# A graph kernel whose first attention block is gathered during the list stage

## The chip, the cores and the metric

The kernel runs on one core of one Trainium2 chip, in one launch. The metric is device time in microseconds (us). A core has TensorE (PE, matmuls), VectorE (DVE), ScalarE (ACT), GpSimd (POOL) and SyncE (SP); each works through its own instructions in order, and semaphores tie them together. Sixteen DMA engines move data between the chip's memory (HBM) and the core's on-chip memory (SBUF); PSUM is the memory that PE writes to. SP and ACT issue plain DMAs. POOL issues indirect ones, called gathers here: a gather fetches, for each of 128 partitions, one row of a table in HBM whose number stands in an index tile.

## The reference

Two graph layers over 4096 nodes with 512 features and an adjacency matrix `adj` of 4096 x 4096 whole numbers, in which about one entry in a thousand is 1, so that a node has some four neighbours.

```python
# layer 0: attention with 8 heads of 64
Wh = jnp.einsum('nf,hfo->hno', x, W)
f1 = jnp.einsum('hno,ho->hn', Wh, a[:, :64]);  f2 = jnp.einsum('hno,ho->hn', Wh, a[:, 64:])
e = jax.nn.leaky_relu(f1[:, :, None] + f2[:, None, :], 0.2)
e = jnp.where(adj[None] > 0, e, -9e15)
out = jnp.einsum('hnm,hmo->hno', softmax(e), Wh)        # heads side by side: 4096 x 512
x = layernorm(x + out)
# layer 1: mean over neighbours
agg = (adj > 0) @ x / max(deg, 1)
out = relu(concat([x @ W_self + b_self, agg @ W_nb + b_nb]) @ W_comb + b_comb)
x = layernorm(x + out)
```

## The kernel before

It never multiplies by the adjacency matrix. It turns each row of the matrix into a short list of neighbours and then gathers only the rows that are listed. (A second function, `dense_layers`, runs only if a list overflows; it does not run on these inputs.) Work is cut into 32 blocks of 128 nodes (`NB`, `P`).

**The list stage** (loop at the end of `listed_layers`, `for b in range(LB)`, 27 steps). A step does three things. It takes a block of x, transposes it on PE (`transposed`, L353, copied out by ACT, L355), multiplies by W (`node_half`, L361), and writes a row of 528 numbers for each node into the HBM table `t0`: 8 numbers f2, 512 of Wh, 8 of f1 (`store`, L970, on POOL's queue; the last block's on SP's). It masks a block of `adj` on ACT (`mask_adj`, L425) from two loads of 1 MB (`load_adj`, L419, on SP), and PE and DVE fold it into keys (`fold_adj`, L444; `max_keys`, L459). And every fourth step, `decode` unpacks four blocks of keys on DVE into lists. In five steps (`AHEAD`) two node blocks are done, so that t0 is written in 27 steps while five adjacency blocks are left; one of them, block 27, is folded just after. The x blocks stay in `xs`, one slot for each, for both layers' residuals; `load_x` (L347) runs eight blocks ahead. POOL copies small parts of each row (`node_rest`, L388 to L390), stores the row, and adds it to a running sum (`add_row`, L398), from which the mean row is made (L408) and stored as the last row of t0; nodes without neighbours point to it.

**Slots.** Block b has `KS` = 5 index columns `idx[:, b, k]`: slot 0 is each node's first neighbour, and slots 1 to 4 are shared: each serves 32 of the block's 128 nodes, and holds their further neighbours packed one after another. Which node owns an entry of a shared slot is a 0/1 matrix (`own`), and a matmul with it adds the entry to its owner.

**Early and late lists.** `late_lists` (L563, on steps 12 to 16) makes second lists for blocks 0 to 5 (`NE`), for layer 1: `idxe` is `idx` with every entry from a limit on replaced by a row of padding, so that layer 1 can gather its first blocks before the last rows are written, and `idxl` is one more slot per block with the neighbours left out, whose owners stand in `esl`. For block 0 the limit is row block 25 (`LE`). In layer 0 these lists are not used.

**Layer 0** (`for i in range(-3, NB + 2)`) is a pipeline written out by hand. Step i gathers block i+6 (L626, five gathers, one for each slot), computes the attention weights of block i+3 (`a_weights`, L658; `a_exp`, L666), multiplies the gathered rows of block i+2 by them (`a_weigh`, L676; `a_first`, L684), adds the shared slots' rows of block i+1 to their owners on PE (`a_shared`, L701, 16 small matmuls) and finishes them with residual and moments (`a_recip`, `a_scale`, `a_moments`, L709 to L723), normalizes block i on ACT (L731 to L740), and multiplies block i-1 by the folded weights of layer 1 (`a_z`, L745), whose result goes to the HBM table `t1` (L750); the transposed block is stored too (L753). There are five gather buffers (`GA`), so the gathers of a block wait until `a_shared` of the block five before is done. Blocks 0, 1 and 2 are gathered before the loop. The four adjacency blocks that are left, 28 to 31, are loaded in quarters of 512 KB into two weight tiles that are still free (`load_late`, L945) and masked (`mask_late`, L961) at the end of the steps that `MASKS` names; after a block's fourth quarter, the next step folds it. After the last of them, `TURN` starts their `decode` and loads the self weights.

**Layer 1** gathers five slots of t1 for each block, with seven buffers (L626 again), blocks 0 to 5 early and with one late slot, and multiplies each block's transposed rows by the folded self weights (L771, into the PSUM tiles `nm` and `pw` in turn) and adds the shared slots to their owners (L778).

The order on each engine is that of the program text (`manual_schedule`); the framework adds the waits. For DMAs of SP and ACT together it has eight semaphores, which are used in turn, so a DMA waits for the one eight before it; POOL's DMAs have eight of their own.

The start sets the first loads. These lines come before the list stage:

```python
    for h in range(H):
        nc.sync.dma_start(
            w_sb[:, :, H + h * D : H + (h + 1) * D], w0[h].rearrange("(c p) o -> p c o", p=P)
        )
    load_x(0, nc.scalar)
    brw = load_bias()
    load_x(1)
    load_adj(0, ap)
```

Of the kernel before, what the change touches and what calls it, by code (L numbers as in the profile page):

```python
# [31 lines left out]
F32 = mybir.dt.float32  # L32
# [81 lines left out]
def listed_layers(  # L114
# [35 lines left out]
    FIRST = (0, 1, 3, *range(LB + 1, NB))  # L150

# [114 lines left out]
    esl = const.tile([P, NE, 2], F32, name="esl")  # L266
    endl = const.tile([P, NE + 8], F32, name="endl")[:, 0:NE]
# [77 lines left out]
    def load_x(b, eng=nc.sync):  # L345
        if b < NB:
            eng.dma_start(xs[:, b, :], x[ts(b, P), :])  # L347
# [215 lines left out]
    def late_lists(dp, place):  # L563

        L = lst[:, 0:NE, 0:KL]
        far = lim.unsqueeze(2)
        lv = dp.tile([P, NE, KL], F32, name="lv", bufs=1)
        nc.vector.tensor_tensor(lv, L, far.to_broadcast([P, NE, KL]), OP.is_ge)
        nl = dp.tile([P, 16], F32, name="nl", bufs=1)[:, 0:NE]
# [8 lines left out]
        tl = dp.tile([P, NE, KL + 3], F32, name="tl", bufs=1)  # L578
        nc.vector.tensor_copy(tl, lst[:, 0:NE, 0 : KL + 3])
# [15 lines left out]
        pe = ps.tile([P, NE, KL + 3], F32, name="sm", bufs=2)  # L595
        for b in range(NE):
            nc.tensor.matmul(pe[:, b, :], lhsT=place[:, b, :], rhs=tl[:, b, :], start=True, stop=True)
        el = dp.tile([P, NE, KL + 3], F32, name="el", bufs=1)
        nc.vector.tensor_copy(el, pe)
        nc.vector.tensor_copy(esl, el[:, :, KL + 1 : KL + 3])  # L600
        kx = dp.tile([P, NE], F32, name="kxl", bufs=1)
# [10 lines left out]
        nc.vector.tensor_scalar(idxl, jx, float(N + 1), None, OP.min)  # L612
# [29 lines left out]

    def gather_early(b, pool):
        return gather(t1[0 : 2 + min(LE + b, LX) * P, :], b, pool, idxe)
# [5 lines left out]
    G0, OWN, E, EX0, RD, Y, NM, MV, RS = ({} for _ in range(9))  # L650
# [4 lines left out]

    def a_weights(b, wp):
        e = E[b] = wp.tile([P, KS + 1, H], F32, name="e", bufs=3)[:, 0:KS]
        nc.vector.tensor_add(e, G0[b][:, :, 0:H], f1s[:, b])  # L658
        nc.vector.scalar_tensor_tensor(e, e, SLOPE, e, OP.mult, OP.max)

    def a_exp(b):

        e = E[b]
        EX0[b] = e[:, 0, :]
        w = E[b] = ps.tile([P, KS, H], F32, name="ew")
        nc.scalar.activation(w, e, AF.Exp)  # L666
        nc.scalar.activation(G0[b][:, K0:KS, 0:H], e[:, K0:KS, :], AF.Exp)
# [28 lines left out]
    def a_shared(b):  # L696

        for a in range(2):
            r = slice(a * (H + HH), H + HH + a * HH)
            for k in range(KH):  # L700
                nc.tensor.matmul(  # L701
                    NM[b][ts(k, HP), a * HD : a * HD + r.stop - r.start],
                    lhsT=OWN[b][:, k, :], rhs=G0[b][:, K0 + k, r],
                    start=False, stop=True, tile_position=(0, k * HP), skip_group_check=True,
                )
# [145 lines left out]
    for h in range(H):  # L851
        nc.sync.dma_start(
            w_sb[:, :, H + h * D : H + (h + 1) * D], w0[h].rearrange("(c p) o -> p c o", p=P)
        )
# [16 lines left out]
    xT = transposed(0, wp)  # L871
# [100 lines left out]
    w, lists = 0, []  # L972
    for b in range(LB):
        for k in range(1 + (b in AHEAD)):
            load_x(w + k + XL)
        if b + 2 <= LB:
            load_adj(b + 2, ap)
        if b == 4:
            pads(wp)
        for k in range(2):  # L980
            some(lists)
        ahead = [transposed(w + 1, wp) if w + 1 < NB else None]
        key_bank(b + 1)
        mask_adj(b + 1, 0)

        def then():
            ahead.append(transposed(w + 2, wp))
            mask_adj(b + 1, 1)

        if b not in AHEAD:  # L990
            mask_adj(b + 1, 1)
        row = node_block(
            w, xT, None if ahead[0] is None else b, keep=ahead[0] is None,
            **(dict(then=then) if b in AHEAD else {}),
        )
        w, xT = w + 1, ahead[0]
        if b in AHEAD:
            node_block(w, xT)
            w, xT = w + 1, ahead[1]
        for k in range(2):  # L1000
            some(lists)
        if b % G == G - 1:
            lists = [decode(b + 1 - G, dp, on_own)]
        if b == 12:
            late_nb = late_lists(dp, last)
        if 12 <= b < 17:
            next(late_nb, None)
# [17 lines left out]

    gps = [gather_buffer(0)]
    G0[0] = gather(t0, 0, gps[0])
# [10 lines left out]
    G0[1] = gather(t0, 1, gps[1])  # L1038
# [14 lines left out]
    G0[2] = gather(t0, 2, gps[2])  # L1053
    MASKS = {-1: 2, 0: 2, 1: 1, 2: 1, 3: 2, 4: 1, 5: 1, 6: 2, 7: 1, 8: 1, 9: 2}
# [8 lines left out]
    biased = fold_bias(loaded, bcol[:, FB:])  # L1063
    for i in range(-3, NB + 2):
        if on(i + 1):
            a_shared(i + 1)
        if on(i + 1 + GA):
            G0[i + 1 + GA] = gather(t0, i + 1 + GA, gps[(i + 1 + GA) % GA])
        elif on(i + GA - NB - 1) and i + GA - NB - 1 < GA:
            b = i + GA - NB - 1  # L1070
            G1[b] = gather_early(b, gps[(NB + b) % GA])
        if on(i + 3):
            a_weights(i + 3, wq)
        if on(i + 2):
            a_weigh(i + 2, slice(K0, KS))
# [36 lines left out]
        for k in range(2 if i == 1 else 0):  # L1112
            load_late()
        for k in range(MASKS.get(i, 0)):
# [21 lines left out]
    gps = [gps[(NB + b) % GA] for b in range(GA)]  # L1136
# [480 lines left out]
```

## Time and profile before

| | us |
|---|---|
| median of the runs (3 runs, 632.29 to 635.61) | 632.58 |
| the profiled execution, its own time | 634.25 |
| its span, first to last instruction | 632.5 |
| list stage, to POOL's first gather | 206.9 |
| POOL's last gather starts | 618.6 |
| busy: PE, DVE, ACT, POOL | 555.4, 427.6, 395.7, 395.5 |

Times in the profile count from the span's start. A row of the timeline gives start, duration, engine, line, operation and tiles, and in brackets the idle time of the engine before it with what ended that time ("issue": nothing that the profile shows). A row of the page's groups gives line, engine, operation, count, then busy time in us and the mean of one in ns, and the idle time before. A row of the rates by stage gives for each engine its busy us and number of instructions, then TensorE's granted clock as a share of full speed, the share of time the DMA engines were busy (a little over 1 where packets overlap), and GB/s. DMA-issuing instructions of SP do not count as busy; a gather's time on POOL does, and is the time to issue it, not to land it.

### The profile page before, as it was taken

To read this page: it belongs to the slowest core of one execution; us is meant where nothing else is said; L and a number is where in the kernel's file an instruction comes from. 1 tells how busy PE (TensorE), PEld (TensorE's weight loads), DVE (VectorE), ACT (ScalarE), POOL (GpSimd) and SP (SyncE) were. 2 spreads that over 40 slices of the span, in tenths; PEclk is the share of its full clock that TensorE was granted. 3 is DMA by queue.
4 is the path that set the end of the run, shared out by engine and by line. 5 is a ranking of instruction groups with operands and counts; after the bars stand their busy time and mean duration, and the time that the engine had idled before them with its cause. 6 is when DMAs were issued, how large, how long until landed. Compare 5 with 4: busy or idle time off the path is not lost.

```text
span 632.5 us, 9237 instructions
## 1 busy us (share of the span) xinstructions
PE 555.4 (88%) x2562; PEld 281.8 (45%) x2562; DVE 427.6 (68%) x1176; ACT 395.7 (63%) x891; POOL 395.5 (63%) x503
## 2 busy tenths in 40 slices
PE   7889799888898397989998989988889999999993
PEld 4666576665665233434443434443433333333321
DVE  7237879899799878768999997794024545455422
ACT  2577777668587036878885757775235666766541
POOL 5235344334444777767777777777777777777771
PEclk9889999999999788989999989999999999999997
DMA  8999999999898978999999999999879999999983
GB/s 230 406 408 377 410 407 408 409 408 409 314 374 314 356 218 276 372 405 404 363 368 391 307 293 312 308 290 307 293 226 308 308 330 317 328 325 322 311 272 124
DMA packets 92107, 210.45 MB, mean 333 GB/s; under 512 B 13761, under 2 KB 13769, under 8 KB 92048
## 3 DMA queue, kind: packets, MB, share of 16 engines
q1 hardware_dynamic: 63296, 114.32, 48.6%
q0 software_dynamic: 28560, 95.17, 44.7%
q8 instruction: 23, 0.38, 0.2%
q10 hardware_dynamic: 192, 0.28, 0.2%
q14 instruction: 36, 0.29, 0.1%
HBM read 175.91 MB, written 33.83 MB: 332 GB/s over the span
## 4 chain that ended last, share of the span: by engine, by line
PE 39%; DMA 26%; DVE 23%; ACT 6%; issue 4%; POOL 1%; SPq 1%; DVEq 0%; ACTq 0%; POOLq 0%
DMA at<-in_adj_dram 12%; DMA g<-t,idx 9%; PE pw L771 8%; PE nm L771 8%; PE pw L745 5%; PE pw L361 4%; DVE g L676 3%; PE nm L778 3%; PE pw L778 2%; PE tp L314 2%; PE pw L314 2%; DMA wc<-in_adj_dram 2%; ACT ab L425 2%; DVE lt L528 2%; DVE kk L459 1%
## 5 line engine op out<-in xcount | busy, mean ns | idle before, releaser
L626 POOL DMA_INDIRECT g<-t,idx x290 | 276.3, 953 | 93.5 <-issue 49.4
L361 PE MATMUL pw<-w_sb,xT 128*128 128x264 f32 x496 | 125.7, 400 | 9.6 <-DVE row L365 9.4
L425 ACT ACTIVATE ab<-at 128x2048 bf16<-128x2048 int32 x56 | 106.8, 1908 | 37.8 <-DMA at<-in_adj_dram 32.5
L745 PE MATMUL pw<-wr,xT 128*128 128x512 f32 x256 | 120.4, 614 | 3.3 <-ACT xT L355 3.2
L361 PEld LDWEIGHTS pw<-w_sb,xT 128*128 128x128 f32 x496 | 91.8, 194 | 35.2 <-DVE row L365 12.8
L676 DVE TENSOR_TENSOR g<-g,ew 128x2048 f32<-128x2048 f32 x32 | 73.0, 2283 | 8.2 <-ACT ew L666 8.2
L388 POOL COPY lst<-row 128x8 f32<-128x8 f32 x32 | 6.9, 215 | 114.1 <-DVE row L365 93.2
L745 PEld LDWEIGHTS pw<-wr,xT 128*128 128x128 f32 x256 | 46.9, 193 | 63.9 <-issue 49.8
L771 PE MATMUL pw<-m,xT 128*128 128x512 f32 x128 | 58.9, 603 | 0.0
L771 PE MATMUL nm<-m,xT 128*128 128x512 f32 x128 | 58.8, 602 | 0.0
L355 ACT COPY xT<-tp 128x512 f32<-128x512 f32 x64 | 37.2, 582 | 19.4 <-PE tp L353 19.3
L353 PE MATMUL tp<-ident,xs 128*128 128x128 f32 x256 | 40.7, 284 | 4.9 <-DVE jk L548 2.3
L365 DVE COPY row<-pw 128x264 f32<-128x264 f32 x62 | 26.3, 425 | 27.7 <-PE pw L361 23.2
L353 PEld LDWEIGHTS tp<-ident,xs 128*128 128x128 f32 x256 | 31.6, 146 | 29.0 <-issue 17.7
L398 POOL TENSOR_TENSOR acc<-acc,row 128x528 f32<-128x528 f32 x30 | 39.6, 1319 | 0.6
L794 DVE SCALAR_TENSOR_TENSOR sm<-g,lst,nm 128x512 f32<-128x512 f32 x15 | 11.3, 755 | 41.1 <-PE nm L778 34.3
L771 PEld LDWEIGHTS pw<-m,xT 128*128 128x128 f32 x128 | 23.2, 189 | 35.3 <-issue 26.9
L771 PEld LDWEIGHTS nm<-m,xT 128*128 128x128 f32 x128 | 23.3, 190 | 34.9 <-issue 25.7
L701 PE MATMUL num<-g,own 128*32 128x256 f32 (+1 forms) x512 | 35.6, 396 | 2.9 <-ACT num L694 2.9
L794 DVE SCALAR_TENSOR_TENSOR sm<-g,lst,pw 128x512 f32<-128x512 f32 x15 | 11.3, 755 | 37.2 <-PE pw L778 33.0
L626 POOL DMA_INDIRECT g<-t,idxe x30 | 28.8, 959 | 9.1 <-issue 5.8
L731 ACT ACTIVATE row<-y,ln_sum 128x512 f32<-128x512 f32 x31 | 22.4, 722 | 15.6 <-DVE y L799 15.6
(233 smaller groups left out, 881.2 us busy)
## 6 DMA issues: line engine op xcount, KB each, us to landing
at<-in_adj_dram SPq DMA_DIRECT2D x56, 1024.0 KB
xt<-xT SPq DMA_DIRECT2D x32, 256.0 KB
t<-row SPq DMA_DIRECT2D x32, 256.0 KB
xT<-xt SPq DMA_DIRECT2D x32, 256.0 KB
out_dram<-row SPq DMA_DIRECT2D x32, 256.0 KB
t<-row POOLq DMA_DIRECT2D x31, 264.0 KB
xs<-in_x_dram SPq DMA_DIRECT2D x31, 256.0 KB
m<-in_adj_dram SPq DMA_DIRECT2D x10, 512.0 KB
```

Of the source, the lines that this page charges most:

```text
L353: nc.tensor.transpose(tp[:, c, :], xs[:, b, ts(c, P)], ident)
L355: nc.scalar.copy(t, tp)
L361: nc.tensor.matmul(pw, lhsT=xT[:, c, :], rhs=w_sb[:, c, k * HW : (k + 1) * HW], start=(c == 0), stop=(c == FB - 1),)
L365: nc.vector.tensor_copy(row[:, k * HW : (k + 1) * HW], pw)
L398: nc.gpsimd.tensor_tensor(acc, acc, row, OP.add)
L425: nc.scalar.activation(ab, loads.pop((b, h)), AF.Relu, accum_out=asum[:, b, h : h + 1])
L626: nc.gpsimd.indirect_dma_start(out=out, out_offset=None, in_=table, in_offset=bass.IndirectOffsetOnAxis(ap=at, axis=0),)
L676: nc.vector.tensor_tensor(gv, gv, E[b][:, sl].unsqueeze(3).to_broadcast([P, sl.stop - sl.start, H, D]), OP.mult,)
L701: nc.tensor.matmul(NM[b][ts(k, HP), a * HD : a * HD + r.stop - r.start], lhsT=OWN[b][:, k, :], rhs=G0[b][:, K0 + k, r], start=False, stop= ...
L745: nc.tensor.matmul(pz, lhsT=xT[:, c, :], rhs=m2[:, c, :], start=(c == 0), stop=(c == FB - 1))
L771: nc.tensor.matmul(NM[b], lhsT=xT[:, c, :], rhs=m1[:, c, :], start=False, stop=(c == FB - 1), skip_group_check=True,)
L778: nc.tensor.matmul(NM[b][ts(k, HP), :], lhsT=OWN[b][:, k, :], rhs=g[:, K0 + k, 0:HD], start=False, stop=True, tile_position=(0, k * HP), s ...
```

## The change

Four things are done together.

1. W is loaded by four DMAs, one for each 128 rows, in place of eight, one for each head.
2. Block 0 of layer 0 (`EB` = 1) is gathered during the list stage, after step 19 and each of the four steps behind it, with the early lists `idxe`. One late slot, with `idxl`, is gathered once t0 is complete; `late_lists` now also carries the first neighbour and f1 of the late entries' owners, and layer 0 gets one more product slot, one more matrix (`a_far`) and two more matmuls for block 0 alone. Its 6 x 528 numbers for each partition lie where x blocks 17 to 23 lie in `xs`.
3. So x blocks 17 to 23 are loaded twice: in the list stage into the slots of blocks 25 to 31, which are loaded in their turn once the first users are transposed, and again into their own slots in steps 2 to 8 of layer 0. The gathers that follow the list stage begin with four slots of block 1, then block 0's late slot, then block 1's first; the buffers go round one block later, and five blocks, 1 to 5, are gathered before a buffer is used again.
4. `MASKS` puts the sixteen late masks on twelve steps, -1 to 10, in place of eleven; `TURN` follows it by one step.

```diff
+    EB = 1
+    XE = NB - XL
+    XG = XE - -(-EB * (KS + 1) * FW // FIN)
...
+    ge = xs.rearrange("p b f -> p (b f)")[
+        :, XG * FIN : XG * FIN + EB * (KS + 1) * FW
+    ].rearrange("p (b k f) -> p b k f", b=EB, k=KS + 1)
...
+    def held(b):
+        return XE + b % XL if XG <= b < XE else b
+
-    def load_x(b, eng=nc.sync):
+    def load_x(b, eng=nc.sync, to=None):
         if b < NB:
-            eng.dma_start(xs[:, b, :], x[ts(b, P), :])
+            eng.dma_start(xs[:, held(b) if to is None else to, :], x[ts(b, P), :])
...
+        tl = dp.tile([P, NE, KL + 3 + H], F32, name="tl", bufs=1)
+        nc.vector.tensor_copy(tl, lst[:, 0:NE, :])
+        nc.vector.tensor_copy(tl[:, :, 0:K0], idx[:, 0:NE, 0:K0])
...
+        nc.vector.tensor_copy(f1l, el[:, 0:EB, KL + 3 :])
...
+    def gather_ahead(n):
+
+        for b in range(EB):
+            for k in (*range(1, KS), 0):
+                while n() < LE + b:
+                    yield
+                rows_of(ge[:, b, k, :], t0[0 : 2 + (LE + b) * P, :], idxe[:, b, k : k + 1])
+                yield
...
+    def slots(b):
+        return KS + (b < EB)
+
+    def a_far(b, wp):
+        OL[b] = wp.tile([P, P], F32, name="ol", bufs=2)
+        nc.vector.scalar_tensor_tensor(
+            OL[b], iota[:, 1 : P + 1], esl[:, b, 1:2], ones, OP.is_equal, OP.mult
+        )
...
-        nc.vector.tensor_add(e, G0[b][:, :, 0:H], f1s[:, b])
+        nc.vector.tensor_add(e[:, 0:KS], G0[b][:, 0:KS, 0:H], f1s[:, b])
+        if b < EB:
+            nc.vector.tensor_add(e[:, KS], G0[b][:, KS, 0:H], f1l[:, b])
...
+            if b < EB:
+                nc.tensor.matmul(
+                    NM[b][:, a * HD : a * HD + r.stop - r.start], lhsT=OL[b],
+                    rhs=G0[b][:, KS, r], start=False, stop=True, skip_group_check=True,
+                )
...
-    for h in range(H):
+    for c in range(FB):
         nc.sync.dma_start(
-            w_sb[:, :, H + h * D : H + (h + 1) * D], w0[h].rearrange("(c p) o -> p c o", p=P)
+            w_sb[:, c, H : H + HD].rearrange("p (h d) -> p h d", h=H),
+            w0[:, ts(c, P), :].rearrange("h p o -> p h o"),
         )
...
-        for k in range(1 + (b in AHEAD)):
-            load_x(w + k + XL)
+        load_x(w + XL)
...
+        if b in AHEAD:
+            load_x(w + 1 + XL)
...
+        if b > 16:
+            for k in range(EB):
+                next(ahead_of, None)
...
     gps = [gather_buffer(0)]
-    G0[0] = gather(t0, 0, gps[0])
+    G0[EB] = gps[0]
+    for k in range(1, KS):
+        rows_of(gps[0][:, k, :], t0[0 : N + 2, :], idx[:, EB, k : k + 1])
+    for b in range(EB):
+        G0[b] = ge[:, b]
+        rows_of(ge[:, b, KS, :], t0[:, :], idxl[:, b : b + 1])
+    rows_of(gps[0][:, 0, :], t0[:, :], idx[:, EB, 0:1])
...
-    MASKS = {-1: 2, 0: 2, 1: 1, 2: 1, 3: 2, 4: 1, 5: 1, 6: 2, 7: 1, 8: 1, 9: 2}
+    MASKS = {-1: 2, 0: 2, 1: 1, 2: 1, 3: 1, 4: 1, 5: 1, 6: 1, 7: 2, 8: 1, 9: 1, 10: 2}
...
-        if on(i + 1 + GA):
-            G0[i + 1 + GA] = gather(t0, i + 1 + GA, gps[(i + 1 + GA) % GA])
+        b = i + 1 + GA + (EB if i < -1 else 0)
+        if on(b):
+            if i < -1 or i >= EB - 1:
+                G0[b] = gather(t0, b, gps[(b - EB) % GA])
...
+        if XG <= XG + i - EB - 1 < XE:
+            load_x(XG + i - EB - 1, to=XG + i - EB - 1)
```

## The prediction

> **What bounds the kernel now.** I read the page first, then GpSimd's (POOL's) timeline, then the chain of waits, then rates by stage. The costliest group of the page is the indirect gathers that POOL issues, one for each slot of each block.
>
> ```profile
> L626 POOL DMA_INDIRECT g<-t,idx x290 | 276.3, 953 | 93.5 <-issue 49.4
> ...
> L626 POOL DMA_INDIRECT g<-t,idxe x30 | 28.8, 959 | 9.1 <-issue 5.8
> ```
>
> With six late ones that makes 326. Their starts in the timeline:
>
> ```profile
> 206.89 1.23 POOL L626 DMA_INDIRECT g<-t,idx  x1 [2.51 <-issue]
> ...
> 274.69 0.95 POOL L626 DMA_INDIRECT g<-t,idx  x1 [0.30 <-issue]
> 275.94 0.95 POOL L626 DMA_INDIRECT g<-t,idx  x1 [0.30 <-issue]
> 280.16 0.94 POOL L626 DMA_INDIRECT g<-t,idx  x1 [3.27 <-ACT last L961]
> ...
> 618.61 0.95 POOL L626 DMA_INDIRECT g<-t,idx  x1 [0.30 <-issue]
> ```
>
> The beat is 1.25 us (0.95 and a gap of 0.30). 325 intervals of 1.25 are 406.3 us and the time from 206.89 to 618.61 is 411.7: POOL stood still for only 5.4 us in two thirds of the run, 2.96 of them at 280.16. So the page's 63% for POOL hides the pacemaker: after 206.89 the end is set by when the first gather starts, how many there are, and where one waits for its buffer. After the last one 13.9 us follow.
>
> A gather buffer is used again five blocks later, so block b waits for the row sums (L701) of block b-5. PE's rows around that one stop:
>
> ```profile
> 262.53 1.08 PE L701 MATMUL num<-g,own 128*32 128x264 f32 x16
> ...
> 267.61 1.08 PE L701 MATMUL num<-g,own 128*32 128x264 f32 x16
> ...
> 272.06 0.38 PE L444 MATMUL pw<-abl,fold 128*32 128x512 bf16 x1 [2.13 <-ACT abl L961]
> ...
> 272.58 5.40 PE L745 MATMUL pw<-wr,xT 128*128 128x512 f32 x8
> ...
> 278.35 1.08 PE L701 MATMUL num<-g,own 128*32 128x264 f32 x16
> ```
>
> These are blocks 4, 5 and 6. Steps 5.1 us long become one of 10.7, because the fold of late block 29 (L444) waits for two mask activations of one step, and the second of these waits for its load; then L745 runs at a granted clock of 0.70.
>
> Before 206.89 the list stage runs. The chain there hangs on the adjacency loads up to 102.6 (its last such link is the first line below) and on DVE, PE and ACT after that. The rates by stage show the one hole in the load stream, at the start, and two stretches that matter later:
>
> ```profile
> 90.46 12.12 DMA at<-in_adj_dram
> ```
>
> ```profile
> 8.00:9.00 1.00, 0.08 (x1) 0.00 (x0) 0.96 (x2) 1.00 (x2) 0.35 (x1) 1.00 0.85 249
> 9.00:10.00 1.00, 0.52 (x3) 0.48 (x4) 0.97 (x2) 0.06 (x1) 1.00 (x1) 1.00 0.56 82
> 10.00:11.00 1.00, 1.00 (x5) 0.94 (x4) 0.97 (x2) 0.00 (x0) 1.00 (x2) 1.00 0.83 244
> ...
> 60.00:80.00 20.00, 16.82 (x97) 12.04 (x96) 17.73 (x54) 14.78 (x19) 7.34 (x15) 1.00 1.05 409
> 164.00:172.00 8.00, 7.04 (x42) 5.24 (x40) 7.48 (x22) 6.32 (x9) 2.64 (x7) 1.00 0.69 256
> ...
> 276.00:312.00 36.00, 34.01 (x194) 15.33 (x193) 29.21 (x57) 31.95 (x94) 25.12 (x27) 0.99 1.04 402
> ```
>
> The last two columns are the DMA share and GB/s. DMA is full from 11 us to 164 and again from 256 to 312.
>
> **The change, part by part.** The sum is made against the profiled execution: span 632.5, its own time 634.25, which is 1.67 above the median of 632.58; I take that off at the end.
>
> W in four loads. The program's waits let eight DMAs of the SP and ACT queues be under way; the ninth waits for the first. With eight loads of W the first x and adjacency loads wait for pieces of W and are issued at 6.99 and 8.15; with four they are issued while W still streams. That fills the hole: against 405 GB/s the rows lack 156+323+161 = 640 KB, and 30 KB of the next microsecond (375), so 1.65 us; between 0 (the stream was not late where it counts) and 2.0 (with the 364 GB/s up to 16 us). I take 1.65, since the chain hangs on these loads until 102.6. W now comes by rows for all heads, so DVE's first product (7.10, needing half of the heads) may wait about 1 us for the last piece; its results are first used at 20.12, which covers it.
>
> [...]
>
> Late lists (L563): two small DVE copies more, near 0.2 us each by L658 (0.20), and wider ones; 0.45 us on a DVE that is busy 18.9 of 20 us there. Ends 0 and 0.6.
>
> Five gathers of block 0 in the list stage: 6.25 us on POOL, one after each row's sum, where POOL's gaps are 5.34, 2.21, 2.81, 3.64 and 4.02 us (before 171.41, 176.30, 181.39, 187.88, 194.19). The first also waits for its row's store to land; behind it in POOL's order stands only the next block's copies at 171.41, some 5 us away. Were this cover gone, DVE's row copies would wait for row buffers. Their 1.35 MB meet DMA at 256 GB/s and later near 400, where ACT waited once for adjacency (0.98 at 184.53): between 0 and 3.3 us (all at 409), I take 0.15. The x loads that must now wait for transposes of blocks 17 to 23 are free by the time SP reaches the adjacency load behind them (transposes of 20 at 126.2, that load at 129.2). List stage: -1.65 +0.45 +0.15 = -1.05.
>
> Gathers after 206.89: block 0 needs one instead of five. 4 x 1.25 = 5.0 us lead. The late slot stands fifth in the queue, just where block 0's last one stood, so block 0 starts no earlier.
>
> Where the lead meets buffers. Block 0 now costs more at the start: a DVE mask row (0.36, as L529), one more add (0.20) and two matmuls of 264 columns (0.40 each, L361), all on the DVE-PE chain that runs from 220 to 257: +1.36; its wider product (2.28 to 2.85) falls into DVE's idle 1.65 before 227.91. Gathers of blocks 7, 8 and 9 start at 252.03, 258.44 and 264.69, and the sums they wait for end at 249.66, 257.12 and 263.61: slack 2.37, 1.31 and 1.08. With 5.0 less and 1.36 more to wait, the lead is gone at block 9, whose gather starts at 264.97, 0.28 after its old time. So POOL stands still there for some 5.3 us.
>
> Masks over twelve steps. The last mask of late block 29 moves from step 3 to step 4, so L701 of block 6 no longer stands behind that fold: 267.61 +1.36 +5.08 = 274.05, ending at 275.1. Block 11's gather would be due at 264.97 + 10 x 1.25 = 277.5 and does not wait. It started at 280.16: -2.7. The later folds (2.4 us each, as at 291.39) move likewise; blocks 12 to 18 had slack of 1.9 to 4.2 and their sums come earlier too. Bounds: 0 (another wait takes its place) and -8.0 (the whole lead kept and the 2.96 gone).
>
> x blocks 17 to 23 again, in steps 2 to 8: 7 x 256 KB = 1.84 MB, on SP at 0.34 us an issue. A step moves five gathers (1.35 MB), two stores (0.52), masks (8 loads of 512 KB in 7 steps: 0.60) and x (0.26): 2.73 MB, at 402 GB/s 6.8 us against a beat of 6.25. The debt is 3.8 us over seven steps. I cost it at nothing: mask loads are issued about 19 us ahead (259.38 for use at 278.98) and landed in 8.5 to 13.1 us in the chain. Without that cover it costs up to 3.8.
>
> [...]
>
> Layer 1 keeps its order. From 582 on its PE waits for gathers again, so a shift of POOL's queue reaches the end whole.
>
> Sum: -1.05 - 2.7 = -3.75: 630.5 for the profiled execution, 628.8 on the median's scale.
>
> **The rivals.** (B) The start of layer 0 gives way: block 1 is gathered four beats earlier, and if the chain to step 0 shortens by 2 us in place of +1.36, gathers 7 to 9 wait 3.3 us less: 625.5. DVE's 1.26 us wait for block 1 at 223.03 speaks for it; PE's fold matmuls, which pace 222 to 257, against. (C) The lead is eaten and the stop at block 11 only moves, since two masks still share a step for blocks 30 and 31: the list stage alone, 631.5. (D) Slower: x again makes the masks' loads late. Once a load takes over 19 us from issue, the fold holds PE, the sums and then POOL; the debt of 3.8 comes in full and the -2.7 is lost: -1.05 + 3.8 = +2.75, 635.3. Full DMA from 256 to 312 speaks for it, the loads' 8.5 to 13.1 us against.
>
> **How the numbers follow.** 0.5% is 3.2 us, about what this kernel's measurement can tell from no change. The likeliest (0.50) is 628.8, its own range 627 to 631; B 0.14, C 0.20, D 0.16. Faster by over 0.5% (below 629.4): 0.36 of the likeliest, B's 0.14: 0.50. Slower (above 635.8): 0.10, from D with a list stage that gains nothing. Within: 0.40. The range 625.0 to 634.8 leaves out the outer half of B and most of D.
>
> **What would show it.** First adjacency load issued near 5 us and no hole at 9 to 10; first gather of block 1 near 205.8; 322 gathers in all, five of them between 160 and 195; stops of POOL at blocks 7 to 9 of some 5 us together and none at 11; last gather near 614.9. The prediction is wrong if POOL stands still elsewhere for more than 2 us, if mask activations wait for loads in steps 7 to 10, or if the list stage ends later than before.

## The result and the profile after

The changed kernel takes 637.41 us (median of 20 executions, 634.65 to 638.94), the kernel before on the same chip 634.45 (20 executions, 631.56 to 639.06). The ratio is 1.0045, with a 95% interval of 1.0027 to 1.0063: slower by about 0.45%, where 628.8 us, a gain of 0.6%, had been forecast. The profiled execution of the changed kernel took 635.27 us with a span of 633.6; that of before had 634.25 and 632.5. So the two traces show 1.1 us of the 3.0 us between the medians; the rest is in executions without a trace, and what is read from the traces below explains the 1.1.

In what follows, line numbers are those of the changed kernel: the gathers are L637 (L626 before), the shared sums L732 (L701), the added matmuls of block 0 L738, the late mask loads L982 (L945), the masks L998 (L961), the folds L454 (L444), the products with layer 1's weights L781 (L745), the matmuls that fold those weights at the start of layer 0 L321 (L314).

The page's costliest group is still the gathers with `idx`; with layer 1's 30 early ones, block 0's five early ones and one late slot, and layer 1's six late ones they are 327, one more than before.

```profile
L637 POOL DMA_INDIRECT g<-t,idx x285 | 270.8, 950 | 100.5 <-issue 46.0
```

POOL's timeline, at each place where it stood still for over 0.5 us after the list stage, and the last gather:

```profile
205.57 1.12 POOL L637 DMA_INDIRECT g<-t,idx  x1 [2.60 <-DMA t<-row]
...
251.73 0.94 POOL L637 DMA_INDIRECT g<-t,idx  x1 [6.74 <-ACT abl L998]
259.19 0.94 POOL L637 DMA_INDIRECT g<-t,idx  x1 [1.51 <-ACT last L998]
303.44 0.94 POOL L637 DMA_INDIRECT g<-t,idx  x1 [0.84 <-ACT last L998]
311.63 0.96 POOL L637 DMA_INDIRECT g<-t,idx  x1 [0.99 <-PE pw L781]
325.08 0.94 POOL L637 DMA_INDIRECT g<-t,idx  x1 [2.50 <-ACT ln_rs L770]
...
619.96 0.95 POOL L637 DMA_INDIRECT g<-t,idx  x1 [0.30 <-issue]
```

The beat is still 1.25 us. The first gather comes 1.32 us earlier than before (206.89), the last one 1.35 us later (618.61). A stop is the idle time less the usual 0.30. The rows at 251.73 and 259.19 (the first gathers of blocks 7 and 8) are 7.65 us of stop, those at 303.44, 311.63 and 325.08 (blocks 15 to 18) are 3.42, and the 2.96 at block 11 are gone: its gather starts at 277.95, where before it was 280.16.

| | us, after against before |
|---|---|
| first gather | -1.32 |
| four gathers fewer behind it, at 1.25 | -5.00 |
| stops at blocks 7 and 8 | +7.65 |
| stop at block 11 gone | -2.96 |
| stops at blocks 15 to 18 | +3.42 |
| all smaller stops (2.07 against 2.51) | -0.44 |
| last gather | +1.35 |

PE's rows for the sums of blocks 4, 5 and 6, which are 5.1 us apart now, and then the fold of late block 30:

```profile
262.46 1.08 PE L732 MATMUL num<-g,own 128*32 128x264 f32 x16
...
267.55 1.08 PE L732 MATMUL num<-g,own 128*32 128x264 f32 x16
...
272.63 1.08 PE L732 MATMUL num<-g,own 128*32 128x264 f32 x16
```

```profile
289.22 1.08 PE L732 MATMUL num<-g,own 128*32 128x264 f32 x16
...
291.06 0.38 PE L454 MATMUL pw<-abl,fold 128*32 128x512 bf16 x1 [0.34 <-ACT abl L998]
294.41 0.58 PE L454 MATMUL pw<-abl,fold 128*32 128x512 bf16 x1 [2.97 <-ACT abl L998]
...
295.35 5.92 PE L781 MATMUL pw<-wr,xT 128*128 128x512 f32 x8
...
301.63 1.08 PE L732 MATMUL num<-g,own 128*32 128x264 f32 x16
```

So the hole that the masks' order closes at late block 29 opens at late block 30: a step of 12.4 us between two sums. What PE waits for there is at the other end of the chain of waits:

```profile
264.28 14.45 DMA m<-in_adj_dram
278.77 0.03 issue
278.80 14.39 DMA wc<-in_adj_dram
293.21 1.16 ACT abl L998 x2
...
295.42 5.86 PE pw L781 x8
...
301.49 14.48 DMA wc<-in_adj_dram
```

From 264.28 to 315.97 three late mask loads make up 43.3 of the chain's 51.7 us: one lands at 278.73, the next leaves at 278.80, lands at 293.2, and its mask frees the fold. SP's queue shows why (the waits of SP between 250 and 325: line, what it waited for, us in total, times, longest; L982 issues mask loads, L357 x loads):

```profile
SPq L982 <- DMA m<-in_adj_dram: 7.3, 3, 2.7
SPq L982 <- DMA wc<-in_adj_dram: 5.5, 2, 3.1
...
SPq L357 <- DMA xs<-in_x_dram: 4.1, 4, 1.2
```

All rows of the kind "waits for a DMA" add up to 34.7 us in these 75: SP stands at the DMA eight places ahead: the load of 278.80 is the eighth DMA behind that of 264.28 and leaves when that one has landed. Mask load 10 of the sixteen (0 to 15) leaves 3.7 us after the start of the mask that frees its tile, load 14 leaves 10.4 us after.

The start and the stretch of layer 0 by stage (the last two columns are the DMA share and GB/s):

```profile
8.00:9.00 1.00, 1.00 (x5) 0.67 (x5) 0.24 (x1) 0.00 (x0) 0.20 (x1) 1.00 1.04 371
9.00:10.00 1.00, 0.53 (x3) 0.43 (x4) 0.98 (x1) 0.59 (x1) 1.00 (x1) 1.00 1.12 346
10.00:11.00 1.00, 1.00 (x5) 0.92 (x4) 0.98 (x1) 0.00 (x0) 1.00 (x1) 1.00 0.97 340
...
276.00:312.00 36.00, 32.69 (x167) 14.59 (x169) 26.97 (x53) 27.99 (x85) 26.25 (x29) 0.91 1.04 407
```

The hole at 9 us is filled (346 GB/s where there were 82). The last adjacency link of the chain starts at 88.23 where it started at 90.46. Between 276 and 312 PE's granted clock is 0.91 where it was 0.99; DMA was and is full (a share of 1.04 in both).

### The profile page after: what moved, and what is told of

It reads as the page before. It is cut to its first block, busy times and chain, and to the rows that moved or that the text cites. A ratio compares the mean times of both kernels' runs of the same rounds, so it can differ in the third digit from the quotient of the medians.

```text
span 633.6 us, 9249 instructions
## 1 busy us (share of the span) xinstructions
PE 561.0 (89%) x2565; PEld 284.5 (45%) x2566; DVE 429.0 (68%) x1180; ACT 395.5 (62%) x891; POOL 396.6 (63%) x504
## 4 chain that ended last, share of the span: by engine, by line
PE 43%; DMA 25%; DVE 22%; ACT 5%; issue 3%; POOL 1%; SPq 0%; DVEq 0%; ACTq 0%; POOLq 0%
DMA at<-in_adj_dram 11%; PE pw L807 9%; PE pw L781 8%; PE nm L807 8%; DMA wc<-in_adj_dram 5%; DMA g<-t,idx 4%; DVE g L707 3%; PE pw L371 3%; PE nm L814 3%; PE pw L321 2%; PE pw L814 2%; PE tp L321 2%; DMA m<-in_adj_dram 2%; PE num L732 2%; DVE row L375 2%
## 5 line engine op out<-in xcount | busy, mean ns | idle before, releaser
L637 POOL DMA_INDIRECT g<-t,idx x285 | 270.8, 950 | 100.5 <-issue 46.0
L781 PE MATMUL pw<-wr,xT 128*128 128x512 f32 x256 | 123.5, 627 | 1.7 <-ACT xT L365 1.5
L781 PEld LDWEIGHTS pw<-wr,xT 128*128 128x128 f32 x256 | 48.2, 198 | 64.9 <-issue 52.8
L707 DVE TENSOR_TENSOR g<-g,ew 128x2048 f32<-128x2048 f32 x31 | 70.7, 2282 | 4.3 <-ACT ew L697 4.3
L732 PE MATMUL num<-g,own 128*32 128x264 f32 (+1 forms) x496 | 34.5, 397 | 2.0 <-ACT num L725 2.0
L637 POOL DMA_INDIRECT g<-t,idxe x30 | 28.8, 960 | 9.1 <-issue 4.0
L785 ACT COPY row<-pw 128x512 f32<-128x512 f32 x32 | 18.7, 583 | 24.9 <-PE pw L781 24.9
```

The costliest lines, as they stand in the source:

```text
L637: nc.gpsimd.indirect_dma_start(out=out, out_offset=None, in_=table, in_offset=bass.IndirectOffsetOnAxis(ap=at, axis=0),)
L707: nc.vector.tensor_tensor(gv, gv, E[b][:, sl].unsqueeze(3).to_broadcast([P, sl.stop - sl.start, H, D]), OP.mult,)
L732: nc.tensor.matmul(NM[b][ts(k, HP), a * HD : a * HD + r.stop - r.start], lhsT=OWN[b][:, k, :], rhs=G0[b][:, K0 + k, r], start=False, stop= ...
L781: nc.tensor.matmul(pz, lhsT=xT[:, c, :], rhs=m2[:, c, :], start=(c == 0), stop=(c == FB - 1))
```

## The experiments

Twelve kernels were run. For seven of them the kernel before took 634 to 636 us on the same chip; for five it took about 750 us, and these are compared with nothing but that and stand together at the end of this section. Of the changed kernel's parts, the suspects were these: the x blocks that are loaded again (their place in SP's order, their number or their bytes), the sums of block 0 at the start, and the masks' order.

### The x load behind the mask load

```diff
-        if XG <= XG + i - EB - 1 < XE:
-            load_x(XG + i - EB - 1, to=XG + i - EB - 1)
...
             full += mask_late(lp)
+        if XG <= XG + i - EB - 1 < XE:
+            load_x(XG + i - EB - 1, to=XG + i - EB - 1)
```

> The x reload of steps 2 to 8 is issued behind the late mask's load of the same step on SP, and in front of nothing of that step. Theory 1 (the x load stands in SP's order in front of the mask load and waits for an old DMA, so loads 10 to 14 leave 3 to 9 us late): loads leave within 1.5 us of the mask activations they follow, no mask activation waits for a load, the sums of blocks 10 to 14 are as early as before and the 3.4 us of POOL's stops at blocks 15 to 18 go: 634 us, ratio to before 0.999. Rival (the 1.84 MB themselves, in a full DMA, make everything late): the stops stay, ratio 1.0045 as for the changed kernel.

Measured: 636.85 against 635.77 us, ratio 1.0017 (0.9998 to 1.0035); last gather at 620.18. From load 11 on the mask loads leave late as before the edit (load 11 at 277.4, 3.7 us behind the start of its mask; load 13 at 292.9, 7.6 behind), SP waits 36.5 us for DMAs, and the stops at blocks 15 to 18 come together in one:

```profile
325.32 0.95 POOL L637 DMA_INDIRECT g<-t,idx  x1 [3.29 <-ACT ln_rs L770]
```

The ratio alone lies between the two forecasts; the trace decides. Theory 1 falls: the order within a step is not the cause, since the next step's mask load stands behind this step's x load anyway.

### The x loads in steps 12 to 18

```diff
-        if XG <= XG + i - EB - 1 < XE:
-            load_x(XG + i - EB - 1, to=XG + i - EB - 1)
+        if XG <= XG + i - 12 < XE:
+            load_x(XG + i - 12, to=XG + i - 12)
```

> The x reload moves from steps 2 to 8 to steps 12 to 18, where no mask load is left. Both theories of the reload (order on SP, or bytes beside the masks) say: loads as prompt as before, no stops at blocks 15 to 18, last gather 3.4 us earlier, ratio 0.999 (634 us); stops at blocks 7 and 8 stay near 7.6 us. If the late loads had nothing to do with the loss (the start chain alone): stops at 15 to 18 stay, 1.0045.

Measured: 632.89 against 635.77, ratio 0.998 (0.9943 to 1.0018), 0.0065 below the changed kernel's ratio, which is 4.1 us (by the two intervals, give or take some 2.6); the last gather starts 4.01 us earlier. POOL's timeline and SP's waits between 250 and 325:

```profile
251.38 0.94 POOL L637 DMA_INDIRECT g<-t,idx  x1 [6.78 <-ACT abl L998]
258.84 0.94 POOL L637 DMA_INDIRECT g<-t,idx  x1 [1.52 <-ACT last L998]
...
615.95 0.94 POOL L637 DMA_INDIRECT g<-t,idx  x1 [0.30 <-issue]
```

```profile
SPq L982 <- ACT abl L998: 2.3, 4, 0.6
...
SPq L982 <- DMA xt<-xT: 1.1, 1, 1.1
```

Nothing stops POOL from block 9 until 384. SP waits 3.9 us for DMAs and not 34.7, a mask load now waits for the mask that frees its tile, and PE's fold of block 30 is done by 292.3 (and L781 behind it takes 3.70 us where it took 5.92):

```profile
291.75 0.38 PE L454 MATMUL pw<-abl,fold 128*32 128x512 bf16 x1 [0.66 <-ACT abl L998]
...
292.27 3.70 PE L781 MATMUL pw<-wr,xT 128*128 128x512 f32 x8
...
296.34 1.08 PE L732 MATMUL num<-g,own 128*32 128x264 f32 x16
```

The x loads of steps 2 to 8 cost the whole of the loss, and more. The stops at blocks 7 and 8 (7.69 us) have nothing to do with them.

### As many x loads, but thin ones

```diff
+    def thin(b):
+        nc.sync.dma_start(xs[:, b, 0:16], x[ts(b, P), 0:16])
...
+        if XG <= XG + i - 12 < XE:
+            load_x(XG + i - 12, to=XG + i - 12)
         if XG <= XG + i - EB - 1 < XE:
-            load_x(XG + i - EB - 1, to=XG + i - EB - 1)
+            thin(XG + i - EB - 1)
```

> Steps 2 to 8 issue their seven x loads at the place and in the number of the changed kernel, but each moves only 16 of 512 columns (8 KB in place of 256); the whole blocks are loaded in steps 12 to 18. Theory bytes (SP's queue gets some 190 GB/s beside the gathers, as in all kernels so far, and the 1.84 MB are too much for it): late loads leave promptly, SP stands still for old DMAs under 5 us between 250 and 325, no stop at blocks 15 to 18, last gather within 1 us of the run with the reload in steps 12 to 18 (615.95), ratio 0.998. Theory count (the eight DMAs that may be under way, whatever they move): loads 10 to 14 leave 3 to 9 us late as in the changed kernel, SP's waits stay near 28 us, last gather near 619.9, ratio 1.003.

Measured: 632.70 against 634.01, ratio 0.998 (0.9955 to 1.0004), last gather at 615.85, no stop over 0.1 us at blocks 15 to 18. So it is the bytes that cost the time. One half of what was expected of them failed: SP still waits 23.5 us for DMAs, and load 11 leaves 3.6 us behind its mask, load 14 5.5 behind. The count alone makes the loads leave late; but what is ahead of them is small, so they land in time: of the masks only the last waits for its load, 0.5 us.

The queues' bytes between 270 and 300 us put this in numbers (packets, MB, share of 16 engines; q0 are the gathers, q1 is the queue of SP and ACT), the changed kernel first, then the one with the x loads in steps 12 to 18:

```profile
q0 software_dynamic: 1962, 6.62, 54.8%
q1 hardware_dynamic: 3020, 5.61, 48.8%
```

```profile
q1 hardware_dynamic: 2982, 5.57, 48.5%
```

Beside the gathers, which take 220 GB/s in both (6.62 and 6.60 MB in 30 us), q1 gets 187 and 186 GB/s: the DMA engines are full in both (409 and 408 GB/s in all), and the gathers give nothing up. In before, where POOL stood still for 2.96 of these 30 us, the gathers moved 5.86 MB and q1 6.25, or 208 GB/s: in these three traces q1 got what the gathers left, 405 to 409 GB/s in all. A step's two stores and one mask load are 1.05 MB, which is 5.6 us at 187 GB/s; with the x block they are 1.31 MB and 7.0 us, while PE does a step in 5.1 us when it catches up and POOL gathers a block in 6.25. And eight DMAs, which is what may be under way, are two steps' worth with an x load in each, 2.62 MB or 14.0 us: the 14.4 us that each load in the chain above takes.

### The mask order of before in the changed kernel

```diff
-    MASKS = {-1: 2, 0: 2, 1: 1, 2: 1, 3: 1, 4: 1, 5: 1, 6: 1, 7: 2, 8: 1, 9: 1, 10: 2}
+    MASKS = {-1: 2, 0: 2, 1: 1, 2: 1, 3: 2, 4: 1, 5: 1, 6: 2, 7: 1, 8: 1, 9: 2}
```

> The changed kernel with the mask order of before (eleven steps). Prediction's theory (two masks of late block 29 in step 3 hold PE at the fold and cost POOL its stop at block 11, 2.96 us): that stop comes back, and the time is 2 to 3 us above the changed kernel, ratio 1.008 to 1.009. Rival (the order of masks moves the stop only, since later folds hold PE for as long): stop at block 11 back, stops at 15 to 18 smaller by as much, ratio 1.0045.

Measured: 638.24 against 635.77, ratio 1.0032 (1.0006 to 1.0057), no higher than the changed kernel's 1.0045. Neither expectation holds in full, but the rival is near. Block 11 has no stop (the gathers are late already by the stops at 7 and 8); one of 2.85 us stands at block 14 instead (at 301.23), and those at blocks 15 to 18 shrink to 0.3.

All stops together are 13.67 us, with twelve steps 13.14, but the difference stands before block 7 (1.66 against 0.97), whose gathers come before the step in which the two orders first differ. At blocks 10 to 18 the stops are 3.35 us in the one and 3.38 in the other: beside the x loads the new order of masks is worth nothing that can be seen.

### The mask order of before, and the x loads in steps 12 to 18

Both edits above together.

> The changed kernel with the x reload in steps 12 to 18 and the mask order of before. With the reload out of the way the masks' worth is seen: by the prediction's working 2.7 us, so last gather near 618.6 against 615.95, ratio 1.002. Rival (the stop is not bound to the mask order, since the stops at blocks 7 and 8 have already made the gathers late enough): last gather within 1 us of 616, ratio 0.998.

Measured: 634.31 against 634.01, ratio 1.0002 (0.9977 to 1.0027), last gather at 618.82, 2.87 later than with twelve steps. Of that, 0.98 is there at the first gather (206.19), where the masks have no part yet; 1.9 are stops (11.38 in all against 9.49): 1.68 at 317.99, in block 17, where twelve steps have none, and 0.3 more before block 7, where the orders don't differ yet.

So without the x loads the masks over twelve steps are worth about 1.7 us, between the two expectations.

### W and the masks alone, on the kernel before

```diff
-    for h in range(H):
+    for c in range(FB):
         nc.sync.dma_start(
-            w_sb[:, :, H + h * D : H + (h + 1) * D], w0[h].rearrange("(c p) o -> p c o", p=P)
+            w_sb[:, c, H : H + HD].rearrange("p (h d) -> p h d", h=H),
+            w0[:, ts(c, P), :].rearrange("h p o -> p h o"),
         )
...
-    MASKS = {-1: 2, 0: 2, 1: 1, 2: 1, 3: 2, 4: 1, 5: 1, 6: 2, 7: 1, 8: 1, 9: 2}
+    MASKS = {-1: 2, 0: 2, 1: 1, 2: 1, 3: 1, 4: 1, 5: 1, 6: 1, 7: 2, 8: 1, 9: 1, 10: 2}
```

> The kernel before with two parts of the change alone: W in four loads and the masks over twelve steps; no early gathers, no second x load. First gather tells W: by the prediction's working 1.65 us earlier than 206.89, so 205.2 (rival: the hole at the start is not what the chain hangs on, 206.9). POOL's stop at block 11 tells the masks: gone, 2.96 us (rival: another stop of the same length behind it). Last gather 618.61 - 1.65 - 2.96 = 614.0, 630 us, ratio 0.993. By the rival for the masks 617.0 and 0.997.

Measured: 630.36 against 634.01, ratio 0.9927 (0.9903 to 0.9952): these two parts alone beat both kernels. First and last gather:

```profile
204.45 1.14 POOL L626 DMA_INDIRECT g<-t,idx  x1 [1.95 <-DMA t<-row]
...
614.78 0.95 POOL L626 DMA_INDIRECT g<-t,idx  x1 [0.30 <-issue]
```

The stop at block 11 is gone: at blocks 10 to 18 the stops are 0.37 us where they were 3.03, so here the order of masks is worth the 2.7 that had been forecast. New are 2.06 us of stops at blocks 7 and 8 (0.84 and 1.22), because gathers that start 2.44 us earlier meet buffers that come free only 0.55 us earlier (sums of block 2 at 248.03 where they were at 248.58). Smaller ones shrink by 0.5.

The changed kernel differs from this one by the early gathers and the second x loads alone. Together these two cost 1.2% by the ratios, and 5.2 us at the last gather (619.96 against 614.78). With the x loads in steps 12 to 18, 1.2 us of that are left (615.95): the first gather is 0.8 later there, four gathers fewer save 5.0, and the stops are 9.49 us in place of 4.08.

### A sixth gather buffer

The x loads stand in steps 12 to 18, so block 0's space is free from step 0 on and can hold blocks 6 and 12.

```diff
+    def in_buffer(b):
+        if b in (6, 12):
+            return ge[:, 0]
+        return gps[(b - 1) % (GA + 1) if b < 13 else (b - 13) % GA]
...
-                G0[b] = gather(t0, b, gps[(b - EB) % GA])
+                G0[b] = gather(t0, b, in_buffer(b))
...
-            G1[b] = gather_early(b, gps[(NB - EB + b) % GA])
+            G1[b] = gather_early(b, gps[(NB - 13 + b) % GA])
...
-        if XG <= XG + i - EB - 1 < XE:
-            load_x(XG + i - EB - 1, to=XG + i - EB - 1)
+        if XG <= XG + i - 12 < XE:
+            load_x(XG + i - 12, to=XG + i - 12)
...
-    gps = [gps[(NB - EB + b) % GA] for b in range(GA)]
+    gps = [gps[(NB - 13 + b) % GA] for b in range(GA)]
```

> As the run with the reload in steps 12 to 18, and block 0's own space then takes blocks 6 and 12 as a sixth gather buffer, so that blocks 7 to 12 wait for sums one step (5.1 us) older. Theory 2 (the lead of the five early gathers is real and only the buffers eat it): the 7.6 us of stops at blocks 7 and 8 shrink below 2.5, last gather 5 to 8 us earlier than without, 627 us, ratio 0.988. Rival (the sums of layer 0 are late anyway and the stop comes back at later blocks): ratio 0.999 as without the sixth buffer.

Measured: 631.15 against 635.77, ratio 0.9926 (0.9895 to 0.9957), faster than both kernels. POOL's timeline at the first gathers of blocks 7, 8 and 9, and the last gather:

```profile
245.27 0.95 POOL L637 DMA_INDIRECT g<-t,idx  x1 [0.30 <-issue]
...
252.02 0.95 POOL L637 DMA_INDIRECT g<-t,idx  x1 [0.30 <-ACT abl L998]
...
259.18 0.95 POOL L637 DMA_INDIRECT g<-t,idx  x1 [0.96 <-issue]
...
611.82 0.95 POOL L637 DMA_INDIRECT g<-t,idx  x1 [0.30 <-DVE sm L830]
```

Of the 7.69 us of stops between blocks 6 and 9, 1.4 are left (0.66 at 259.18, and 0.48 and 0.24 inside blocks 7 and 8); 1.3 come back at blocks 15 to 18, which is the rival's part. From the first gather to the last POOL stands still for 4.8 us, where the run with five buffers has 9.5 and the kernel before 5.5. So most of the lead is there to be had once a buffer is free for it: the last gather starts 4.1 us earlier than with five buffers. In its trace the span is 625.7 us, 6.8 below before; the ratio of the medians says 4.6 us, and the forecast 0.988 lies outside its interval. Against W and the masks alone the trace is 3.0 us earlier at the last gather (611.82 against 614.78), but the ratio is the same (0.9926 against 0.9927): that the early gathers gain anything over those two parts, even with a sixth buffer, is not shown by the times.

### Five runs where the kernel before took 750 us

Four kernels, among them the three above with edits of the x loads and the buffers, had first been run on another chip, where the kernel before itself took 749.58 us, and the last run fell on such a chip too (753.38 for before). There POOL stands still at nearly every block. The rates between 300 and 350 us, with the x load behind the mask load, on that chip; and then the changed kernel on its own:

```profile
300.00:350.00 50.00, 40.40 (x196) 17.04 (x196) 29.45 (x59) 31.88 (x97) 27.83 (x30) 0.90 0.92 301
```

```profile
300.00:350.00 50.00, 46.28 (x259) 20.88 (x258) 39.77 (x84) 37.15 (x114) 35.10 (x38) 0.97 1.03 391
```

301 GB/s against 391, with the DMA engines busy 92% of the time. What takes the bandwidth isn't in the traces. With it the stops of a few us that these runs were to tell apart drown among some 100 us of others. Two ratios lie just above 1, for W in four loads and for the x loads in steps 12 to 18; why, these traces do not tell, and no gain is shown on such a chip.

W in four loads alone, on the kernel before:

> The kernel before with W in four loads and nothing else of the change. Theory (the list stage hangs on its first loads): the hole in the load stream at 9 to 10 us is filled, the first gather starts 1.3 to 1.7 us earlier than before (about 205.4), everything behind shifts with it, and the time is 1.3 to 1.7 us lower (ratio 0.997 to 0.998). Rival (the gain is eaten by DVE and PE between 103 us and the first gather, or by waits behind it): first gather within 0.5 us of before, or earlier with no change of the time (ratio 1.000).

Measured 752.13, ratio 1.0063 (1.0006 to 1.012); first gather at 204.96, 1.9 us earlier than in the trace of before above; the time does not show it.

The x loads in steps 12 to 18:

> The changed kernel with the second loads of x 17 to 23 in steps 12 to 18 in place of 2 to 8, behind the last mask. Theory (these loads make the late masks' loads late, the folds of blocks 30 and 31 wait for them, and POOL stops at blocks 15 to 18): mask loads are issued within 1 us of the mask before them, the waits of ACT for masks 11, 14 and 15 and POOL's 3.4 us of stops at blocks 15, 16 and 18 go, the stops at blocks 7 and 8 (7.6 us) stay; time 3 to 4 us below the changed kernel, ratio to before 0.997 to 1.000. Rival (DMA is full and the bytes only collide elsewhere): the same stops come in steps 12 to 18 and the ratio stays at 1.004.

Measured 751.57, ratio 1.0067 (1.0007 to 1.0127).

The sixth buffer:

> As the run before (second x loads in steps 12 to 18), and block 0's gather space serves as a sixth gather buffer for blocks 6 and 12, so that blocks 7 to 12 wait for the block six before them. Theory (the lead of four gathers is lost because buffers come back too late at the start): the stops at blocks 7 and 8 shrink from 7.6 us to under 2, the last gather starts 5 to 7 us earlier than in the run before, ratio to before 0.986 to 0.992. Rival (not the buffers but the chain of PE, DVE and ACT paces this stretch, so that gathers only wait later): stops of about the same sum at blocks 13 to 18, time within 1.5 us of the run before.

Measured 746.30, ratio 0.9968 (0.9911 to 1.0026).

The x load behind the mask load:

> The changed kernel with each second x load behind its step's mask and mask load in SP's order, in the same steps 2 to 8, the same bytes. Theory S (SP stands at the x load, which waits for the DMA eight before it, and the mask load behind it is issued 3 to 9 us late): mask loads 11 to 15 are issued within 2 us of their masks, the folds' waits shrink, time 2 to 3 us below the changed kernel. Theory B (bandwidth: the queue of SP gets under 190 GB/s and seven more loads are too much whatever their order): mask loads are issued or land as late as in the changed kernel, fold waits of about 5 us stay, ratio 1.003 to 1.006.

Measured 748.36, ratio 0.9985 (0.992 to 1.005).

The sixth buffer with the mask order of before:

> The run with six gather buffers and the reload in steps 12 to 18, with the mask order of before. Theory (a fold that holds PE costs POOL something only where the gather behind it has no slack; with a sixth buffer blocks 7 to 12 wait for sums a step older, and slack is over 5 us there): last gather within 1 us of 611.8, ratio 0.992. Rival (the two masks of one step cost their 2.7 us wherever the gathers stand): last gather near 614.5, ratio 0.997.

Measured 757.33 against 753.38; POOL's stops add up to over 100 us. Whether the masks' order still matters with six buffers stays open.

## Why the prediction was wrong

Step by step, in its order.

**The x loads, costed at nothing: the step that failed.** The prediction worked out that a step would need 6.8 us of DMA against a beat of 6.25, and let a cover of 19 us from issue to use hide that. Their cost is 4.0 us (last gather 619.96 against 615.95 with nothing but their place changed; 4.1 us by the ratios), at its upper bound of 3.8 or a little above. Two things in the reasoning were off. The debt was shared out over all DMA, 402 GB/s; but the gathers kept their beat, so all of it fell on SP's queue, at 187 GB/s, and there a step needs 7.0 us in place of 5.6, beside a beat of 6.25 for POOL and steps of 5.1 for PE. And the cover was read from before as if it were a constant: a load is issued when the DMA eight places ahead has landed, so as soon as that queue is the slower one, each load leaves when an older one lands, and the cover shrinks with each step: 19 us from issue to use in before, 14.4 for load 11. That is rival D's mechanism. D's number, +2.75 (635.3), is also near the +2.96 of the medians, but partly by luck: D adds 3.8 for the x loads and 2.7 for the lost gain of the masks. Measured, the two are one loss of 4.0: the x loads cost their time at the fold of late block 30, and the stop at block 11 stayed away all the same. The stops at blocks 7 and 8, 7.65 us in place of 5.3, which D did not have, make up for most of what it counts twice.

**Masks over twelve steps, -2.7.** The place was right: PE's sums of blocks 4 to 6 are 5.1 us apart, the stop of 2.96 at block 11 is gone, and its gather started at 277.95. The size is 2.7 us on the kernel before with W in four loads, 1.7 behind early gathers with the x loads out of the way, and nothing beside the x loads: there the next fold becomes late in its turn.

**The lead of the early gathers, eaten at blocks 7 to 9.** Right in kind: all five of them are issued between 167 and 189 us, and the 5.0 us are gone by block 8. Too small in size: stops of 7.65 us, not 5.3. The sums of block 2, for which block 7's gather waits, were due 0.31 us later than before (+1.36 of start chain, -1.05 of list stage), and came 1.34 later (they end at 251.00, before at 249.66). The start chain, from the first weights of block 0 (e) to the sums of block 2, is 30.71 us (219.21 to 249.92) where it was 27.91 (220.67 to 248.58): +2.80, not +1.36. The PE rows of the run with the x loads in steps 12 to 18, where the chain is 30.82, name the parts:

```profile
220.72 5.54 PE L321 MATMUL pw<-wc,row 128*128 128x512 f32 x8 [6.56 <-ACT row L310]
...
230.56 0.65 PE L732 MATMUL num<-xs,own 128*32 128x264 f32 x8
231.14 0.71 PE L738 MATMUL num<-xs,ol 128*128 128x264 f32 x2
...
232.89 0.60 PE L309 MATMUL pw<-ident,wr 128*128 128x128 f32 x4
...
242.86 6.35 PE L321 MATMUL pw<-wc,row 128*128 128x512 f32 x8
```

and the same group of before:

```profile
242.94 5.27 PE L314 MATMUL pw<-wc,row 128*128 128x512 f32 x8
```

The sums of block 0 take 2.33 us until the next group in place of 1.01: +1.32, where two matmuls at 0.40 had been put at 0.80 (the two halves are 1.29 us long with them). The two groups of eight L321 matmuls that follow an idle PE take 5.54 and 6.35 in place of 5.28 and 5.27, +1.3: the second has a granted clock of 0.61 between 246 and 249, where it was 0.96. The prediction had nothing for that. The mask row, put at 0.36 on the path, stands just ahead of e, where DVE was idle before (0.49 us), and does not lengthen this chain. A gather also starts 0.73 us behind the end of the sums it waits for, in before as in after (279.43 to 280.16, 251.00 to 251.73); measured from that gate, the slack at blocks 8 and 9 was 0.58 and 0.35, not 1.31 and 1.08.

**List stage, -1.05.** The first gather comes 1.32 us earlier, the last adjacency link 2.2. In the seven kernels with W in four loads and the early gathers, outside the five runs at 750 us, it stands between 204.43 and 206.45, so one trace can't settle a term of 1 us. The rates between 8 and 11 us rise by 122, 264 and 96 GB/s, which is 482 KB or 1.2 us, not 1.65: the hole is filled to 340 to 371 GB/s, not 405, and the microsecond behind it loses 43 KB (332 GB/s for 375). The first adjacency load left at 6.35 us (8.15 before), not near 5.

**Layer 1 and the tail.** The beat stays, and the last gather is followed by 13.6 us (13.9 before), as it had been put.

**Put together.** The two parts from which the sum was made, W and the masks, came out as forecast when they were run alone: -3.83 at the last gather, where the sum was -3.75. Some of that is luck, as the list stage gained 2.44 and not 1.05, and blocks 7 and 8 took 1.9 of it back. The two parts put at nothing were what failed:

| | us at the last gather | us by the ratios |
|---|---|---|
| W and masks alone, against before | -3.83 | -4.6 |
| early gathers added (x loads in steps 12 to 18) | +1.17 | +3.4 |
| x loads in steps 2 to 8 | +4.01 | +4.1 |
| the changed kernel, against before | +1.35 | +2.9 |

The first column is differences of single traces, whose first gathers scatter by up to 2 us; the intervals of the ratios leave some 2 to 3 us either way to each row of the second but the last. The x loads are the larger and the better shown of the two. Without them the kernel still falls short of the forecast ratio of 0.994: it has 0.998, as it has with the thin loads.

Beside q1, with its 187 of 409 GB/s, the gathers lost nothing: they held 220 GB/s and their beat of 1.25 us, as they did with the x loads in steps 12 to 18 (220 GB/s beside 186), and it was the other queue that had to be priced.

## What to carry to other kernels

Extra bytes in a full DMA have to be charged to the queue that carries them, at the rate that this queue gets beside the others, and per step: here 1.31 MB at 187 GB/s in place of 1.05 cost 4.0 us, and the same bytes ten steps later cost nothing that can be seen. A time from issue to use that is read in the trace of before is no cover for them if the issue itself waits for earlier DMAs of that queue. And work done ahead is worth what the next shared resource lets through: five early gathers gained nothing with five buffers, and rather cost time; with a sixth, POOL's stops at blocks 7 to 9 fell from 7.69 to 1.4 us. Last, parts that are changed together are best also run apart: W and the masks alone take 0.7% off, and the other two parts took it away again.

## What the runs showed of the hardware

A wait of 3 us cost PE 2.2 us more behind it. In the changed kernel PE was idle for 2.97 us from 291.44 on; the granted clock fell from 1.00 (288 to 292) to 0.63 and 0.52, and the eight L781 matmuls took 5.92 us in place of 3.70:

```profile
288.00:292.00 4.00, 3.10 (x29) 1.26 (x29) 2.98 (x6) 3.01 (x9) 3.09 (x4) 1.00 1.03 402
292.00:296.00 4.00, 1.59 (x6) 0.61 (x6) 2.35 (x8) 2.70 (x8) 3.09 (x4) 0.63 1.05 415
296.00:300.00 4.00, 4.00 (x6) 1.57 (x5) 3.54 (x6) 1.38 (x6) 3.09 (x4) 0.52 1.04 406
```

That a mask late by 2.2 us made PE's sums late by 4.9 (301.63 against 296.34 in the run with the x loads moved, with sums 0.35 apart one step earlier) is this clock and the wait together: 2.3 us for the later start of the fold, 2.2 for L781 and 0.4 for the fold itself. In quarters of a microsecond this trace has the clock at 1.00 until 293.0, at 0.50 from 293.25 to 299.75 and at 1.00 again from 300.0. So it fell 1.6 us into the idle time, and rose some 5.4 us after PE had begun to work at 294.41.

And the number of DMAs and their bytes act apart: seven DMAs of 8 KB made SP wait 23.5 us for older ones, against 3.9 without them, and cost no time that can be measured (ratio 0.998 with them and without).
